# Moving VectorE work in the first and last quad of a gated cross-attention kernel

## The chip, the cores and the metric

The kernel runs on one core of a Trainium2 chip. The metric is the device time of one execution in microseconds, given as the median of several runs. A core has five engines that work side by side, each through its own instructions in order: TensorE (PE: matmuls, with the weight loads shown apart as PEld), VectorE (DVE), ScalarE (ACT), GpSimd (POOL) and SyncE (SP), which here issues most DMA transfers. They wait for each other by semaphores.

## The reference, cut to what matters

x holds 8 batches of 1024 rows with 1024 elements. The memory has 64 rows of 512 elements for each batch. All is float32.

```python
memory_proj = einsum('bme,de->bmd', memory, W_mem)
scores = einsum('bnd,bmd->bnm', x, memory_proj) / sqrt(D)
attn = softmax(scores, axis=-1)
memory_context = einsum('bnm,bmd->bnd', attn, memory_proj)
gate_input = concatenate([x, memory_context], axis=-1)
gate = sigmoid(einsum('bnf,df->bnd', gate_input, W_gate) + b_gate)
fused = x + gate * memory_context
out = fused * rsqrt(mean(square(fused)) + EPS) * norm_w
```

Softmax subtracts the row's maximum before the exponential. W1 below is the half of W_gate that meets x, W2 the half that meets the context.

## The kernel before, in words

**Tiling.** The 8192 rows of x are worked in 16 quads of 512 rows (four tiles of 128 rows, t = 0 to 3). A setup of about 80 us computes the projected memory and its product with W2 and stores both to DRAM. Then each quad multiplies its rows by W1 in a Strassen-like scheme with two levels: seven outer products, taken in ORDER 1, 6, 7, 5, 4, 2, 3 (line 613), each of seven inner products. An inner product is one call of `product` (line 866) and one slot, so a quad has 49 slots.

**One outer product** (`outer_product`, line 855) uses PSUM banks af and ed (two sets, in turn), and b and c. Its first inner product goes to af and is copied by ScalarE (line 876). The second, kB, goes to bank b and is drained by VectorE into u2. The third, kC, goes to bank c and is drained into u3. The fourth and fifth end in ed, drained into u4; the sixth and seventh in af. GpSimd's `pre` adds u3 and u4 to the gate tiles of 128x512, and VectorE's `fin_af` and `fin_ed` add the banks. L95 is the helper `tt` for all two-operand sums, L92 the helper of all matmuls, L98 that of SP's transfers.

**The visit.** Products 5 and 4, and products 2 and 3, form pairs. After kC of the second of a pair (4 or 3), TensorE makes a visit (line 796): the context itself and its part of the gate, for both of the pair, into banks b and c, two further banks, and af and ed. The first matmul of the visit needs bank b, so VectorE's drain of kB must have ended. After the visit come bank sums, the sigmoid on ScalarE, and the multiplication by the context (`gated`, or `last_gated` in the last quad, which also adds x from xl).

**Softmax.** In slot 10 `softmax_a` takes the row maximum on VectorE (line 429), multiplies it by -SCALE (line 430), and ScalarE takes four exponentials with that as bias. In slot 13 `softmax_b` takes a reciprocal on VectorE and scales on ScalarE. In slot 18 TensorE transposes the weights (line 451).

**Inner sums of W1.** For every outer product the weights have four sums (T1, T2, R12, T4, lines 214 to 216). Those of products 2 and 3 are not made in the setup: VectorE makes them in the first quad, in slots 3, 4, 5, 6 for product 2 and 12, 14, 16, 18 for product 3 (line 656). R12 is overwritten in place.

**The last quad.** Its tiles are finished by `last_square` (sum of squares, ScalarE), `last_root` (square root, ScalarE) and `last_norm`: a reciprocal on VectorE, one VectorE operation per half tile (multiply by the reciprocal root, multiply by norm_w), and a store of that half on SP. The list `when` (line 940) sets the slots for a pair: roots of tiles d and c, then norms (d, 0), (d, 1), (c, 0), (c, 1). For product 4 the tiles are d = 3 and c = 2; None stands for a place in the middle of product 3, right after its visit.

**Order.** The program is its own schedule: `at(slot, ...)` puts a step ahead of the inner product of that slot, `mid((quad, product), ...)` behind the bank sums that follow a visit, `mid((quad, product, 0), ...)` between the visit and these sums. `pin` keeps each engine's instructions in program order. An instruction that waits holds up all behind it on its engine.

Of the kernel before, what the change touches and what calls it, by code (L numbers as in the profile page):

```python
# [9 lines left out]
AF = mybir.ActivationFunctionType  # L10
ALU = mybir.AluOpType
# [9 lines left out]
def tile_gated_cross_attention_rmsnorm(  # L21
# [42 lines left out]
    nc = tc.nc  # L64
# [4 lines left out]
    NQ = B * QPB  # L69
# [3 lines left out]
    H = 512  # L73
    C = 256
    NPAIR = BM // P
    SCALE = 1.0 / float(D) ** 0.5
# [12 lines left out]
    pin = tc.keep_in_program_order  # L89
# [4 lines left out]
    def tt(eng, o, a, b, op):  # L94
        pin(eng.tensor_tensor(o, a, b, op))  # L95

    def load(o, i):
        pin(nc.sync.dma_start(o, i))  # L98

    def t4k(pool, shape, tag, name):  # L100
        return pool.tile(shape, F32, tag=tag, name=name)
# [31 lines left out]
    for k in range(KD):  # L133
        t = t4k(*((gpool, [P, D], "gate") if k < 7 else (apool, [P, D], "s4")), f"w2_{k}")
# [8 lines left out]
    nw_sb = const.tile([P, D], F32, name="nw_sb")  # L143
# [194 lines left out]
    A, S, L2, O = {}, {}, {}, {}  # L338
    sTs, attns, attnTs, scs, dens, mps, mgs = {}, {}, {}, {}, {}, {}, {}
    def where(q, t=0):  # L340
        return q // QPB, (q % QPB) * QT + t * P
# [84 lines left out]
    def softmax_a(q):  # L426
        sc = scs.pop(q)
        mx = t4k(small, [P, 4], "mx", f"mx{q}")
        pin(nc.vector.tensor_reduce(mx, sc, AX.X, ALU.max))
        pin(nc.vector.tensor_scalar(mx, mx, -SCALE, None, ALU.mult))  # L430
        e = attns[q] = t4k(small, [P, 4, M], "e", f"e{q}")
        den = dens[q] = t4k(small, [P, 4], "den", f"den{q}")
        for t in range(4):
            pin(
                nc.scalar.activation(
                    e[:, t], sc[:, t], AF.Exp, bias=mx[:, t : t + 1], scale=SCALE, accum_out=den[:, t : t + 1]
                )
            )
# [167 lines left out]
    def at(slot, fn, *args):  # L606
        due.setdefault(slot, []).append(lambda: fn(*args))

    def mid(key, fn, *args):
        beside.setdefault(key, []).append(lambda: fn(*args))  # L610
# [5 lines left out]
    def plan(q):  # L616
# [11 lines left out]
        at(t0 + (11 if q else 22), outer_s, q, 4)  # L628
        at(t0 + 9, transpose_scores, q)
        at(t0 + 10, softmax_a, q)  # L630
        at(t0 + 13, softmax_b, q)
        at(t0 + 18, transpose_attn, q)
# [20 lines left out]
    for o in (2, 3):  # L653
        w1_place(o)
    for i, (o, n) in enumerate((o, n) for o in (2, 3) for n in range(4)):
        at((3, 4, 5, 6, 12, 14, 16, 18)[i], inner_sum, nc.vector, o, n)
    slot = 0

    def step():
# [88 lines left out]
    def last_root(t):  # L748
# [5 lines left out]
            )  # L754
        )

    def last_norm(t, h):
        b, n0 = where(NQ - 1, t)
        rstd = halves[t][0][:, 2:3]
        if h == 0:  # L760
            pin(nc.vector.reciprocal(rstd, rstd))
        cols = slice(h * H, (h + 1) * H)
        g = O[NQ - 1, t][:, cols]
        pin(
            nc.vector.scalar_tensor_tensor(g, g, rstd, nw_sb[:, cols], ALU.mult, ALU.mult)  # L765
        )
        load(out[b, n0 : n0 + P, cols], g)

    def sqrt_table():

        t = t4k(small, [P, 1], "warm", "warm")
        pin(nc.scalar.activation(t, eps_sb, AF.Sqrt))
# [82 lines left out]
    def outer_product(q, o):  # L855
# [66 lines left out]
        if second:  # L922
            row, h, _ = EXT[o]
# [12 lines left out]
        if second and not nxt:  # L936
            c, d = 2 * row, 2 * row + 1
            if o == 3:
                sqrt_table()
            when = (3, 4, 5, 6, None, 11) if o == 4 else (0, 2, 2, 2, 3, 3)  # L940
            at(slot + when[0], last_root, d)
            at(slot + when[1], last_root, c)
            for w_, (t, h_) in zip(when[2:], ((d, 0), (d, 1), (c, 0), (c, 1))):
                if w_ is None:
                    mid((q, 3, 0), last_norm, t, h_)
                else:
                    at(slot + w_, last_norm, t, h_)
        elif second:

            c, d = 2 * row, 2 * row + 1  # L950
            for t in (d, c):
                at(slot + 5, residual, q, t)
            if row == 0:
                when = (17, 18, -1, None, 33, -2) if q + 2 < NQ else (17, 18, 20, 22, 24, 25)
            else:
                when = (17, 18, 22, 24, 29, 31)
            at(slot + when[0], square, q, c)
            at(slot + when[1], square, q, d)
            for w_, (t, h_) in zip(when[2:], ((c, 0), (c, 1), (d, 0), (d, 1))):
                if w_ is None:  # L960
                    mid((q + 1, 4), norm, q, t, h_)
                elif w_ < 0:
                    mid((q + 1, 4, 0) if w_ == -1 else (q + 1, 3), norm, q, t, h_)
                else:
                    at(slot + w_, norm, q, t, h_)
        del L2[q, o]

    for q in range(NQ):
        plan(q)
        for o in ORDER:  # L970
            outer_product(q, o)
# [29 lines left out]
```

## Time and profile before

| | us |
|---|---|
| median of 3 runs | 961.03 |
| the three runs | 960.99, 962.22, 961.03 |
| profiled execution | 961.78 |
| its span, first to last instruction | 960.0 |
| TensorE busy | 944.4 |
| VectorE busy | 817.3 |
| GpSimd busy | 712.2 |
| ScalarE busy | 366.3 |

Times in the timelines are microseconds from the first instruction: start, duration, engine, line of the kernel, operation, names of the output and inputs, shape, count, and in brackets how long the engine had been idle and what ended the idle time. Durations of neighbours overlap a little. A busy TensorE is not one at its peak, and the ends of matmuls are modelled. The first quad's products run from about 80 to 142 us, a later quad takes about 54 us, and the last matmul starts at 948.3.

### The profile page before, as it was taken

The page shows a single profiled execution, that of the slowest core. Times are in us where ns is not written, and L with a number is a line of the kernel's source. Part 1 is how long each engine was busy: PE and PEld are TensorE (multiplying, and loading weights), DVE is VectorE, ACT ScalarE, POOL GpSimd, SP SyncE. Part 2 cuts the span into 40 slices and gives each one's busy share as a digit, 9 for nine tenths or more (in the row PEclk, how much of TensorE's full clock was granted, in tenths as well). Part 3 has the DMA queues.
Part 4 walks back from the last instruction along what each step waited for, and adds up shares of the span by engine and source line. Part 5 has one row for each costly group of instructions (what it writes and reads, how often), then busy time and mean ns, then how long its engine had stood idle before and what let it go on. Part 6 is the DMA issues. An engine that isn't in the chain of part 4 may idle for free.

```text
span 960.0 us, 14298 instructions
## 1 busy us (share of the span) xinstructions
PE 944.4 (98%) x4984; PEld 777.6 (81%) x4984; DVE 817.3 (85%) x1260; ACT 366.3 (38%) x779; POOL 712.2 (74%) x778
## 2 busy tenths in 40 slices
PE   9999999999999999999999999999999999999994
PEld 7546788888888888888888888888888888888883
DVE  6989878888888888988888888988888888978887
ACT  3000335262433535262433535262433525262454
POOL 4997867788677777787677777777677877777681
PEclk9999999999999999999999999999999999999998
DMA  9866674481919365481919365481919365481712
GB/s 378 268 153 155 108 126 106 104 182 44 209 45 189 91 141 118 109 177 43 210 45 189 88 142 120 101 185 40 213 45 187 87 145 121 107 180 40 203 66 89
DMA packets 70919, 128.33 MB, mean 134 GB/s; under 512 B 12352, under 2 KB 49216, under 8 KB 70592
## 3 DMA queue, kind: packets, MB, share of 16 engines
q1 hardware_dynamic: 61664, 93.86, 37.0%
q0 software_dynamic: 9184, 33.56, 19.1%
q8 instruction: 40, 0.66, 0.3%
q14 instruction: 31, 0.25, 0.1%
HBM read 87.56 MB, written 41.68 MB: 135 GB/s over the span
## 4 chain that ended last, share of the span: by engine, by line
PE 92%; DVE 4%; ACT 1%; issue 1%; POOL 1%; DMA 1%; SPq 0%; POOLq 0%; DVEq 0%; ACTq 0%
PE af L92 28%; PE ed L92 19%; PE pc L92 11%; PE kC L92 9%; PE kB L92 9%; PE psT L92 6%; PE pg L92 5%; PE pm L92 2%; DVE gate L95 1%; DVE u L95 1%; DMA wm<-in_w_mem_t 1%; POOL l L95 0%; DVE gate L765 0%; DVE gate L699 0%; PE sc L420 0%
## 5 line engine op out<-in xcount | busy, mean ns | idle before, releaser
L95 POOL TENSOR_TENSOR gate<-gate,u 128x512 f32<-128x512 f32 (+1 forms) x224 | 248.9, 1123 | 193.9 <-DVE u L95 180.0
L670 ACT ACTIVATE gate<-gate 128x512 f32<-128x512 f32 x128 | 79.8, 630 | 184.2 <-DVE gate L95 184.2
L352 DVE STREAM_TRANSPOSE a<-xq 128x512 f32<-128x512 f32 x128 | 141.0, 1105 | 3.3 <-POOL it L95 3.3
L95 POOL TENSOR_TENSOR l<-a 128x256 f32<-128x256 f32 x128 | 111.9, 874 | 18.7 <-PE af L92 17.5
L699 DVE SCALAR_TENSOR_TENSOR gate<-gate,ss,nw_sb 128x512 f32<-128x512 f32 x120 | 120.7, 1007 | 1.1
L92 PE MATMUL pc<-mg,attnT 64*128 64x256 f32 x512 | 119.0, 383 | 2.2 <-DVE u L95 2.2
L92 PE MATMUL kB<-it,l 128*128 128x256 f32 x448 | 115.1, 379 | 0.5 <-DVE u L95 0.5
L92 PE MATMUL ed<-it,l 128*128 128x256 f32 x448 | 115.0, 379 | 0.0
L92 PEld LDWEIGHTS pc<-mg,attnT 64*128 64x128 f32 x512 | 93.2, 187 | 22.9 <-DVE u L95 13.0
L876 ACT COPY u<-af 128x256 f32<-128x256 f32 x112 | 40.7, 363 | 185.6 <-PE af L92 185.2
L95 DVE TENSOR_TENSOR gate<-gate,pc 128x512 f32<-128x512 f32 x113 | 76.0, 683 | 33.2 <-ACT gate L670 33.1
L92 PE MATMUL af<-w,a 128*128 128x256 f32 x384 | 98.5, 379 | 0.0
L92 PEld LDWEIGHTS kB<-it,l 128*128 128x128 f32 x448 | 85.1, 190 | 12.3 <-issue 0.8
L92 PEld LDWEIGHTS ed<-it,l 128*128 128x128 f32 x448 | 83.9, 190 | 10.7
L95 DVE TENSOR_TENSOR gate<-gate,ed 128x512 f32<-128x512 f32 x112 | 76.1, 680 | 14.4 <-POOL gate L95 14.3
L95 POOL TENSOR_TENSOR l<-s 128x256 f32<-128x256 f32 x96 | 85.1, 886 | 3.0 <-PE af L92 3.0
L92 PEld LDWEIGHTS af<-w,a 128*128 128x128 f32 x384 | 73.0, 190 | 10.3 <-issue 0.5
L95 DVE TENSOR_TENSOR gate<-gate,af 128x512 f32<-128x512 f32 (+1 forms) x128 | 76.0, 604 | 2.1 <-POOL gate L95 1.4
L92 PE MATMUL af<-mg,attnT 64*128 64x256 f32 x256 | 68.8, 389 | 0.0
L92 PE MATMUL ed<-it,a 128*128 128x256 f32 x256 | 67.4, 386 | 0.0
L684 ACT ACTIVATE junk<-gate 128x1024 f32<-128x1024 f32 x60 | 63.5, 1058 | 6.9 <-DMA gate<-in_x 6.0
L92 PE MATMUL af<-t,s 128*128 128x256 f32 x256 | 65.8, 380 | 0.0
(138 smaller groups left out, 1993.5 us busy)
## 6 DMA issues: line engine op xcount, KB each, us to landing
xq<-in_x SPq DMA_DIRECT2D x64, 512.0 KB, 10.4
gate<-in_x POOLq DMA_DIRECT2D x60, 512.0 KB, 8.5
out<-gate SPq DMA_DIRECT2D x60, 512.0 KB, 3.4
w<-in_w_gate_t SPq DMA_DIRECT2D x8, 512.0 KB, 10.2
w<-in_w_gate_t SPq DMA_DIRECT2D x2, 2048.0 KB, 16.1
mg<-mgd SPq DMA_DIRECT2D x16, 256.0 KB, 5.9
wm<-in_w_mem_t SPq DMA_DIRECT2D x4, 512.0 KB, 6.4
mpd<-mpT SPq DMA_DIRECT2D x4, 512.0 KB, 7.0
```

Of the source, the lines that this page charges most:

```text
L92: pin(nc.tensor.matmul(o, lhsT, rhs, start=start, stop=stop, skip_group_check=True))
L95: pin(eng.tensor_tensor(o, a, b, op))
L352: nc.vector.transpose(A[key][:, :, r * P : (r + 1) * P], chunks(xq[q][:, 4 * t : 4 * t + 4, :], KD)[:, half * KH : (half + 1) * KH],)
L670: pin(nc.scalar.activation(g, g, AF.Sigmoid))
L684: nc.scalar.activation(junk, O[q, t], AF.Square, accum_out=ss[:, t % 2 : t % 2 + 1])
L699: nc.vector.scalar_tensor_tensor(g[:, cols], g[:, cols], rstd[:, t % 2 : t % 2 + 1], nw_sb[:, cols], ALU.mult, ALU.mult,)
L876: pin(nc.scalar.copy(p1, af[:, 0]))
```

## The change

It has three parts. First, the multiplication of the row maximum by -SCALE goes from VectorE to ScalarE, in all 16 quads. Second, the four inner sums of W1 for product 3 in the first quad go from slots 12, 14, 16 and 18 to later places: two behind the bank sums after the visit of product 4, and two to slots 33 and 35. Third, in the last quad, tile 2 is multiplied by norm_w by GpSimd (a new step `last_weigh`, one instruction per half, between product 3's visit and the bank sums) and by its reciprocal root by ScalarE, in place of one VectorE operation per half. The new `when` takes the root of tile 2 and the norm (3, 0) in the same slot, puts the norm (3, 1) in the middle of product 3, where (2, 0) was, and the norm (2, 0) in slot offset 10.

```diff
-        pin(nc.vector.tensor_scalar(mx, mx, -SCALE, None, ALU.mult))
+        pin(nc.scalar.activation(mx, mx, AF.Copy, scale=-SCALE))
...
-        at((3, 4, 5, 6, 12, 14, 16, 18)[i], inner_sum, nc.vector, o, n)
+        if i in (4, 5):
+            mid((0, 4), inner_sum, nc.vector, o, n)
+        else:
+            at((3, 4, 5, 6, None, None, 33, 35)[i], inner_sum, nc.vector, o, n)
...
+    def last_weigh(t, h):
+        cols = slice(h * H, (h + 1) * H)
+        g = O[NQ - 1, t][:, cols]
+        tt(nc.gpsimd, g, g, nw_sb[:, cols], ALU.mult)
+
...
-        pin(
-            nc.vector.scalar_tensor_tensor(g, g, rstd, nw_sb[:, cols], ALU.mult, ALU.mult)
-        )
+        if t == 2:
+            pin(nc.scalar.activation(g, g, AF.Copy, scale=rstd))
+        else:
+            pin(
+                nc.vector.scalar_tensor_tensor(g, g, rstd, nw_sb[:, cols], ALU.mult, ALU.mult)
+            )
         load(out[b, n0 : n0 + P, cols], g)
...
-            when = (3, 4, 5, 6, None, 11) if o == 4 else (0, 2, 2, 2, 3, 3)
+            when = (3, 4, 4, None, 10, 11) if o == 4 else (0, 2, 2, 2, 3, 3)
+            if o == 4:
+                for h_ in range(2):
+                    mid((q, 3, 0), last_weigh, c, h_)
```

## The prediction

> **What bounds the kernel now.** I read the page first: busy times, the slices with the clock, then the chain of waits.
>
> ```profile
> span 960.0 us, 14298 instructions
> ...
> PE 944.4 (98%) x4984; PEld 777.6 (81%) x4984; DVE 817.3 (85%) x1260; ACT 366.3 (38%) x779; POOL 712.2 (74%) x778
> ```
>
> TensorE is busy for 944.4 of 960.0 us (98%), and its granted clock stands at 9 tenths or more in every slice but the last. Work taken from another engine pays only where TensorE waits for that engine, or after its last matmul. The TensorE timeline tells where. The first three rows are the first quad, the next two the second quad at the same place as reference, the last two the last quad. The bracket is idle time and its releaser.
>
> ```profile
> 109.87 1.10 PE L92 MATMUL kB<-it,l 128*128 128x256 f32 x4 [0.45 <-DVE u L95]
> 111.19 1.10 PE L92 MATMUL kC<-t,l 128*128 128x256 f32 x4 [0.21 <-DVE u L95]
> 112.75 0.48 PE L92 MATMUL pc<-mg,attnT 64*128 64x256 f32 x1 [0.46 <-DVE u L95]
> ...
> 164.98 1.03 PE L92 MATMUL kB<-it,l 128*128 128x256 f32 x4
> ...
> 166.80 0.48 PE L92 MATMUL pc<-mg,attnT 64*128 64x256 f32 x1
> ...
> 938.92 1.03 PE L92 MATMUL kC<-w,l 128*128 128x256 f32 x4
> 941.33 0.48 PE L92 MATMUL pc<-mg,attnT 64*128 64x256 f32 x1 [1.38 <-DVE u L95]
> ```
>
> Undisturbed, kB to visit takes 166.80 - 164.98 = 1.82 us. In the first quad the product before kB starts at 108.40, so kB was due 0.86 later at 109.26 and the visit at 111.08; it came at 112.75: **1.67 us lost**. In the last quad kC starts at 938.92, the visit was due 0.96 later (166.80 against kC's 165.84), at 939.88, and came at 941.33: **1.45 us lost**. From 113 to 923 no TensorE row carries such a wait. At 923.94 there is one of 0.34 us that the change does not touch.
>
> Next the VectorE timeline, what made it late: first quad, then last.
>
> ```profile
> 93.63 2.23 DVE L430 TENSOR_SCALAR mx<-mx 128x4 f32<-128x4 f32 x1
> ...
> 96.70 0.84 DVE L95 TENSOR_TENSOR it<-w 128x512 f32<-128x512 f32 x1
> ...
> 100.28 0.89 DVE L95 TENSOR_TENSOR it<-w,it 128x512 f32<-128x512 f32 x1
> ...
> 938.36 2.58 DVE L765 SCALAR_TENSOR_TENSOR gate<-gate,halves,nw_sb 128x512 f32<-128x512 f32 x2
> ...
> 941.91 1.79 DVE L765 SCALAR_TENSOR_TENSOR gate<-gate,halves,nw_sb 128x512 f32<-128x512 f32 x1
> ...
> 946.32 0.75 DVE L765 SCALAR_TENSOR_TENSOR gate<-gate,halves,nw_sb 128x512 f32<-128x512 f32 x1
> ```
>
> The four sums of W1 for product 3 (first and last shown, the others at 98.12, 0.68 us, and 99.35, 0.69 us) and the factor stand ahead of the drain of kB at 109.31. In the last quad two norms stand ahead of the drain at 940.86 that frees the visit's bank, and a third ahead of the bank sums at 943.61. From there VectorE works almost without a gap to its last norm at 955.78.
>
> [...] the norm at 941.91 takes 1.79 us with GpSimd's 1.27 us sum started at 941.88, and 0.75 us at 946.32 with GpSimd idle. The factor on 128x4 takes 2.23 us between GpSimd sums. [...] the trace has loads of 1.28 us. [...] the copy of line 876 runs at 903.34, after a Sqrt, with no load before it.
>
> **The change, part by part.**
>
> First quad, removed from ahead of the late drains: the factor's 2.23 us and four sums, 0.84 + 0.68 + 0.69 + 0.89 = 3.10 us. That is 5.3 us, but waits for data take a part. My replay of VectorE's order: u4 of product 6 must wait for its matmuls (about 94.5). The next sum waits for GpSimd's 128x512 sum, done at about 95.5[...]. u4 of product 7 waits for TensorE at 100.8. Then the transposes (next x landed by 87.7 + 12.2 = 99.9) and the rest follow, and the drain of kB of product 5 comes at 107.2 instead of 109.31. The lead of 2.1 us exceeds the 1.67 us needed; product 4's kB is then drained as soon as TensorE delivers it. Take 1.67; at the low end, [...]1.0.
>
> Where the sums go: two stand behind the four bank sums of product 4's visit, ahead of the two multiplications by pc of product 5 (116.73). They cost 0.7 to 1.3 us each. Those multiplications free banks b and c for product 2's kB and kC, TensorE at 120.98 and 121.85. With TensorE 1.67 us earlier and the multiplications done near 117.4, over 2 us remain before 119.3 and 120.2. The other two sums fall where VectorE already waits 0.69 and 0.70 us for a sigmoid (120.50, 122.49). All four are read only in product 3, from about 125. Cost: nothing, with that cover; without it, at most the 3.1 us again.
>
> The factor on ScalarE, 16 times: VectorE loses 0.78 us a quad (2.23 in the first), ScalarE gains 0.2 to 0.3 us (a 128x1 activation takes 0.29 at 931.15). ScalarE idles about 3.9 us before it in each later quad (58.6 us in 15 waits), so nothing is queued behind. The table load then follows the new instruction instead of VectorE's, and the exponentials start 0.5 us earlier. TensorE does not wait here: 0 us on the path from the second quad on.
>
> Last quad. One norm of tile 3 moves ahead of u4 of product 2, the other behind product 3's visit; both norms of tile 2 leave VectorE. Ahead of the late drain stands one norm instead of two. It starts beside GpSimd's sum at 938.00, so I price it 0.75 to 1.79 us against 2.50 for two (938.36 to 940.86): the drain comes 0.7 to 1.75 us earlier, TensorE can use at most 1.45. At the visit one norm replaces a reciprocal and a norm: 0.2 us more. Later the 946.32 norm goes (0.66 from start to start) and tile 2's reciprocal comes back (0.2). VectorE reaches the last bank sum (949.55) 0.7 + 0.2 + 0.46 = 1.4 to 1.45 + 0.2 + 0.46 = 2.1 us earlier. TensorE's last product ends 0.85 us before that sum and moves up too, so it sets no later end.
>
> Cover for the new work: GpSimd weighs twice at 1.27 us (its price at 941.88) in its 5.65 us of idleness ahead of 948.79. ScalarE scales twice at 0.63 (a 128x512 sigmoid)[...], in gaps of 0.88 and 0.94 us before 946.43 and 948.42. Behind the second scaling wait a square and the sigmoid of 949.38: about 0.1 us may be late. [...] I take 1.6 for the tail, 0.5 to 2.2 with these. The stores on SP keep their order; tile 2's come earlier than the last tile's, which alone lie at the end.
>
> Sum: 1.67 + 1.6 = 3.3 us. The profiled span 960.0 becomes 956.7. The profiled execution took 961.78 in all, 1.8 outside its span, and the median of the runs is 961.03: predicted 961.03 - 3.3 = **957.7 us**.
>
> **The rivals.**
> Only one place yields (0.20). For: VectorE's margins are small; after the repair the drain before the visit has only some 0.3 us. Against: 5.3 us are removed for a need of 1.67. Time 961.03 minus 1.4 to 1.7: 959.3 to 959.6, or 958.8 if half of the other comes too.
> No gain (0.09). [...] Against: the weighing has to end only by 948.79. Time 960.3 to 961.5.
> Slower (0.06). The factor on ScalarE lengthens softmax. In the second quad ScalarE's last scaling ends at 154.76, and TensorE's transposes of the weights follow at 155.26, weights loaded at 155.04: a margin of 0.28 us, 15 times. It decides once the chain grows by more than 0.28 us. A second table load in each quad would do so: 1.28 + 0.29 - 0.78 - 0.28 = 0.5 us times 15 = 7.6, less 3.3: 965.3 us. Against: copies after Sqrt and Exp in this trace need no load.
>
> **How the numbers follow.** Both places repaired has 0.65, with its own range 956.7 to 958.7 (1.67 + 2.2 at best, and 0.4 us for run-to-run scatter; 1.0 + 1.4 at worst). Change below 0.2%, 1.9 us, is what a measurement of this kernel cannot tell from none: faster ends at 959.1, slower begins at 963.0. Faster: 0.65 plus half the one-place case, 0.75. Same: the other half and no gain, 0.19. Slower 0.06. The range 956.7 to 959.7 takes in both places and one.
>
> **What would show it.** TensorE rows at kB, kC and the visit of the first quad, about 109.3 to 111.1, without brackets; the last visit within 2.2 us of its kB. If kB still waits there, my replay of the lead is wrong. The transposes of line 451 without a wait, and table loads no more than now. GpSimd's two weighings ended before its last sum; the last bank sum 3.1 to 3.8 us earlier than 949.55. The prediction is wrong if new TensorE waits stand near 119 to 125 or in every quad.

## The result, and the profile after

The changed kernel takes a median of 958.3 us (six runs, 957.75 to 958.74), the kernel before in six runs on the same chip 961.51 (960.99 to 962.22). The ratio is 0.9966, 95% interval 0.9955 to 0.9976: 3.2 us less, 3.3 were forecast. The forecast of 957.7 started from 961.03, so the median lies 0.6 above it. The profiled execution after took 957.75 us, span 956.0. The two spans lie 4.0 us apart, more than the medians; the run "The kernel before once more" shows why.

The page after: span and busy times, the shares of the chain that ended last, and one group of matmuls.

```profile
span 956.0 us, 14301 instructions
...
PE 943.6 (99%) x4984; PEld 778.2 (81%) x4984; DVE 811.4 (85%) x1242; ACT 371.0 (39%) x797; POOL 717.3 (75%) x780
...
PE 97%; DVE 1%; DMA 1%; ACT 0%; issue 0%; POOL 0%; SPq 0%; DVEq 0%
...
L92 PE MATMUL pc<-mg,attnT 64*128 64x256 f32 x512 | 119.0, 383 | 0.3 <-DVE u L95 0.3
```

TensorE's share of the chain is 97%. VectorE lost the 16 factors and two norms (1260 to 1242 instructions), ScalarE gained those 18. The matmuls of the visits wait 0.3 us for VectorE in the whole kernel: that is the untouched wait at product 4's visit in the last quad.

The TensorE timeline after, at the rows that carried brackets before: first quad, then last quad.

```profile
109.08 1.03 PE L92 MATMUL kB<-it,l 128*128 128x256 f32 x4
109.95 1.03 PE L92 MATMUL kC<-t,l 128*128 128x256 f32 x4
110.90 0.48 PE L92 MATMUL pc<-mg,attnT 64*128 64x256 f32 x1
...
937.07 1.03 PE L92 MATMUL kC<-w,l 128*128 128x256 f32 x4
938.03 0.48 PE L92 MATMUL pc<-mg,attnT 64*128 64x256 f32 x1
```

None of these rows waits. kB to visit takes 110.90 - 109.08 = 1.82 us, as in the undisturbed quad that the prediction read.

The VectorE timeline after: the drain of kB of product 5 in the first quad, then the tail of the last quad.

```profile
107.26 0.42 DVE L95 TENSOR_TENSOR u<-u,kB 128x256 f32<-128x256 f32 x1
...
935.39 1.79 DVE L776 SCALAR_TENSOR_TENSOR gate<-gate,halves,nw_sb 128x512 f32<-128x512 f32 x1
...
937.43 0.41 DVE L95 TENSOR_TENSOR u<-u,kB 128x256 f32<-128x256 f32 x1
...
938.48 0.75 DVE L776 SCALAR_TENSOR_TENSOR gate<-gate,halves,nw_sb 128x512 f32<-128x512 f32 x1
...
945.51 0.69 DVE L95 TENSOR_TENSOR gate<-gate,af 128x512 f32<-128x512 f32 x1 [0.75 <-PE af L92]
```

In the last quad one norm stands ahead of the drain (937.43), and the last bank sum (945.51) now waits 0.75 us for TensorE's last product.

To compare runs I measured distances in each trace: from the first matmul of the first quad's first outer product to the first visit; between the last two visits (product 4's and 3's of the last quad); and from the last visit to the last bank sum and to the end of the span. All in us, one execution each. The ends of matmuls are modelled, so only starts of matmuls are used.

| kernel | first visit | between last two visits | last bank sum | end |
|---|---|---|---|---|
| before, profile shown | 32.77 | 17.39 | 8.22 | 18.67 |
| before, profiled again | 32.78 | 16.61 | 8.23 | 18.69 |
| after | 31.10 | 15.94 | 7.48 | 17.92 |
| sums alone | 31.10 | 16.62 | 8.24 | 18.72 |
| factor alone | 32.61 | 16.62 | 8.23 | 18.68 |
| sums and factor | 31.10 | 16.61 | 8.23 | 18.68 |
| last quad alone | 32.69 | 15.94 | 7.48 | 17.94 |
| new order, no hand-over | 31.10 | 15.94 | 8.08 | 18.55 |
| hand-over, old order | 31.10 | 17.40 | 9.69 | 20.12 |
| one half tile more handed over | 31.10 | 15.94 | 7.66 | 18.12 |

### The profile page after: what moved, and what is told of

Read it like the earlier page. It is cut to its first block, busy times and chain, and to the rows that moved or that the text cites. A ratio compares the mean times of both kernels' runs of the same rounds, so it can differ in the third digit from the quotient of the medians.

```text
span 956.0 us, 14301 instructions
## 1 busy us (share of the span) xinstructions
PE 943.6 (99%) x4984; PEld 778.2 (81%) x4984; DVE 811.4 (85%) x1242; ACT 371.0 (39%) x797; POOL 717.3 (75%) x780
## 4 chain that ended last, share of the span: by engine, by line
PE 97%; DVE 1%; DMA 1%; ACT 0%; issue 0%; POOL 0%; SPq 0%; DVEq 0%
PE af L92 30%; PE ed L92 21%; PE pc L92 12%; PE kC L92 10%; PE kB L92 10%; PE psT L92 6%; PE pg L92 5%; PE pm L92 2%; DMA wm<-in_w_mem_t 1%; PE pa L451 0%; PE sc L420 0%; DVE gate L702 0%; DVE gate L776 0%; DVE u L95 0%; DVE gate L95 0%
## 5 line engine op out<-in xcount | busy, mean ns | idle before, releaser
L95 POOL TENSOR_TENSOR gate<-gate,u 128x512 f32<-128x512 f32 (+1 forms) x224 | 243.2, 1098 | 184.4 <-DVE u L95 148.5
L702 DVE SCALAR_TENSOR_TENSOR gate<-gate,ss,nw_sb 128x512 f32<-128x512 f32 x120 | 115.6, 964 | 1.1
L95 POOL TENSOR_TENSOR l<-s 128x256 f32<-128x256 f32 x96 | 78.4, 817 | 3.0 <-PE af L92 3.0
L95 DVE TENSOR_TENSOR u<-u,kC 128x256 f32<-128x256 f32 x112 | 45.9, 410 | 23.8 <-PE kC L92 20.3
```

The costliest lines, as they stand in the source:

```text
L702: nc.vector.scalar_tensor_tensor(g[:, cols], g[:, cols], rstd[:, t % 2 : t % 2 + 1], nw_sb[:, cols], ALU.mult, ALU.mult,)
```

## The experiments

The medians of the kernel before, on the same chip as each run, lie between 961.27 and 961.45 us. Each run below names its own ratio to it.

**The sums alone.** The kernel before with the new places for the four sums, nothing else:

```diff
-        at((3, 4, 5, 6, 12, 14, 16, 18)[i], inner_sum, nc.vector, o, n)
+        if i in (4, 5):
+            mid((0, 4), inner_sum, nc.vector, o, n)
+        else:
+            at((3, 4, 5, 6, None, None, 33, 35)[i], inner_sum, nc.vector, o, n)
```

> Only the four inner sums of W1 for product 3 move, as in the change; factor and last quad as before. My theory: the sums (3.1 us) make most of VectorE's lateness, since the factor's 2.23 us partly overlap waits for data. The drain of kB of product 5 comes 1.6 to 2.0 us earlier than 109.31, TensorE's three waits in the first quad vanish, time -1.5 us (-1.2 to -1.7). Rival, both edits are needed because GpSimd and TensorE data set the pace: -0.8 us or less, with a wait left at the visit. The last visit stays at 1.45 us late in both.

Measured: 959.78 us, ratio 0.998 (0.9971 to 0.9989), 1.5 us less. Its TensorE timeline, where the three waits stood:

```profile
109.59 1.03 PE L92 MATMUL kB<-it,l 128*128 128x256 f32 x4
110.45 1.03 PE L92 MATMUL kC<-t,l 128*128 128x256 f32 x4
111.41 0.48 PE L92 MATMUL pc<-mg,attnT 64*128 64x256 f32 x1
```

The first visit comes 31.10 us after the quad's first matmul: the whole 1.67 us is back with the sums alone.

**The factor alone.**

```diff
-        pin(nc.vector.tensor_scalar(mx, mx, -SCALE, None, ALU.mult))
+        pin(nc.scalar.activation(mx, mx, AF.Copy, scale=-SCALE))
```

> Only the factor moves to ScalarE, in all quads. My theory: the sums then fill the idle time that the factor left[...], so the lead is about 0.7 us: one or two of the three waits in the first quad remain, time -0.7 us (-0.3 to -1.2). In later quads nothing on TensorE: the transposes of line 451 get 0.6 us more room. Rival, the factor alone is the cause: -1.7 us. Rival, a longer softmax chain: TensorE waits at line 451 in each quad, time +7 us.

Measured: 961.06 us, ratio 0.9996 (0.9988 to 1.0005). Its TensorE timeline still has all three waits:

```profile
109.54 1.10 PE L92 MATMUL kB<-it,l 128*128 128x256 f32 x4 [0.27 <-DVE u L95]
110.86 1.10 PE L92 MATMUL kC<-t,l 128*128 128x256 f32 x4 [0.21 <-DVE u L95]
112.43 0.48 PE L92 MATMUL pc<-mg,attnT 64*128 64x256 f32 x1 [0.47 <-DVE u L95]
```

A miss: 0.7 us was expected, the first visit comes 0.16 us earlier, and the median can't be told from no change. Its VectorE timeline where the factor stood, and the first of the four sums:

```profile
94.41 0.42 DVE L95 TENSOR_TENSOR u<-u,ed 128x256 f32<-128x256 f32 x1 [0.97 <-PE ed L92]
95.73 0.69 DVE L95 TENSOR_TENSOR gate<-gate,ed 128x512 f32<-128x512 f32 x1 [0.90 <-POOL gate L95]
96.33 1.27 DVE L95 TENSOR_TENSOR it<-w 128x512 f32<-128x512 f32 x1
```

Of the 2.23 us taken away 0.97 comes back as a wait for TensorE and 0.90 as one for GpSimd. The four sums then took 1.27, 1.24, 0.88 and 0.68 us, 4.07 together against 3.10 before. These three outweigh the 2.23 us; a little is left because a later wait of VectorE for GpSimd shrinks from 1.51 to 0.83 us.

**Both first-quad parts.**

> Factor and sums move, last quad as before. My theory: -1.7 us, no TensorE wait in the first quad, last visit still 1.45 us late. Together with the run of the last quad alone this should sum to the whole change (about -3.2 us) if the two places are independent; if the first place's gain were lost on the way, this run would be at 0.

Measured: 959.36 us, ratio 0.9975 (0.9966 to 0.9985), 1.9 less; first visit at 31.10, as with the sums alone. In the two profiled executions 0.18 us of the difference lies in the setup (the quad's first matmul stands at 80.31 with the sums alone, at 80.13 here); the rest of the 0.4 us between the medians is not tied to a place in the traces, and I take it for scatter.

**The last quad alone.** The changed kernel with the factor and the sums as before.

> Only the last quad's part: order of norms, GpSimd weighing, ScalarE scaling. My theory: from the trace of the changed kernel, TensorE's last visit 1.45 us earlier and the last bank sum 2.2 us earlier, time -2.2 us (the prediction's term was -1.6, its range -0.5 to -2.2). The three waits of the first quad stay at 1.67 us. Rival, the tail is worth only the 1.5 that the medians leave after the first quad: -1.5 us.

Measured: 959.88 us, ratio 0.9984 (0.9976 to 0.9992), 1.4 less, not the 2.2 expected. Against the repeated profile of before, the last visit comes 16.61 - 15.94 = 0.67 us earlier and the end 18.69 - 17.94 = 0.75 nearer to it: 1.42. With both first-quad parts' 1.9 the medians add up to 3.3, against 3.2 for the whole change, so the two places are independent within the scatter.

**The kernel before once more**, unchanged.

> The kernel before, unchanged, for a second trace. In the profile of before, VectorE's first add of xl in the last quad took 1.84 us[...]; in the five other traces the same two operations start as close and VectorE goes first, 0.69 us. If that is an even race of one place, this trace has VectorE first, the visits of products 4 and 3 lie 16.6 us apart (17.4 in the profile of before), and the last visit is 0.7 us late in place of 1.45. If the old program always loses it: 17.4 again.

It took 961.17 us, span 959.4, and shows where the missing 0.8 us went. Its last visit waits 0.60 us where it waited 1.38 in the profile of before:

```profile
940.71 0.48 PE L92 MATMUL pc<-mg,attnT 64*128 64x256 f32 x1 [0.60 <-DVE u L95]
```

The cause shows in the timelines of VectorE and GpSimd in the last quad, first in the profile of before that the prediction read:

```profile
928.53 1.84 DVE L95 TENSOR_TENSOR gate<-gate,xl 128x512 f32<-128x512 f32 x1
928.54 1.27 POOL L95 TENSOR_TENSOR gate<-gate,u 128x512 f32<-128x512 f32 x1
```

Then in the second execution of the same kernel:

```profile
928.69 0.69 DVE L95 TENSOR_TENSOR gate<-gate,xl 128x512 f32<-128x512 f32 x1
928.72 1.79 POOL L95 TENSOR_TENSOR gate<-gate,u 128x512 f32<-128x512 f32 x1
```

The same two operations start within 0.03 us of each other. In the first execution GpSimd's sum takes 1.27 us and VectorE's addition of xl 1.84, in the second GpSimd's takes 1.79 and VectorE's 0.69. Where VectorE loses, that is, where its addition is the long one, the last visit comes 17.39 - 16.61 = 0.78 us later. So the 1.45 us wait that the prediction wanted to recover was 0.67 us of order and 0.78 us of what happened in that one execution. VectorE won in 10 of the 14 traces of this study. The two spans differ by more than the medians for this reason: 959.998 - 955.953 is 4.05, and 4.05 - 0.78 = 3.27 us, of which 0.18 lies in the setup (79.98 against 79.80). The six runs of before fit: three at 960.99 to 961.25 and three at 961.78 to 962.22, with a median between the two groups. Only one of them, at 961.78, has a trace, so the groups are not shown to be the two outcomes.

**The new order without the hand-over.** The changed kernel, but tile 2's norms stay on VectorE, at the new places in `when`:

```diff
-            if o == 4:
-                for h_ in range(2):
-                    mid((q, 3, 0), last_weigh, c, h_)
...
-        if t == 2:
-            pin(nc.scalar.activation(g, g, AF.Copy, scale=rstd))
-        else:
-            pin(
-                nc.vector.scalar_tensor_tensor(g, g, rstd, nw_sb[:, cols], ALU.mult, ALU.mult)
-            )
+        pin(
+            nc.vector.scalar_tensor_tensor(g, g, rstd, nw_sb[:, cols], ALU.mult, ALU.mult)
+        )
```

> The whole change but for the hand-over of tile 2: its norms stay on VectorE, one operation per half, at the new places in the order. My theory: the new order alone repairs the last visit (its first matmul within 1.85 us of kB's), but VectorE carries two operations of 0.66 us more before the last bank sum[...]: last bank sum 0.3 to 0.6 us later after the visit than in the changed kernel (7.48), time -2.7 us against before. Rival, the hand-over is what matters: -1.7 us, as with the first quad alone.

Measured: 958.86 us, ratio 0.997 (0.996 to 0.9979), 2.4 less. The visit is on time (15.94), so the order repairs it. The last bank sum stands 8.08 after it, not 7.48: two norms of 0.75 and 0.74 us are back ahead of the drain that GpSimd's last sum needs. The hand-over is worth these 0.60 us (0.56 by the medians).

**The hand-over with the old order.** One line of the changed kernel undone:

```diff
-            when = (3, 4, 4, None, 10, 11) if o == 4 else (0, 2, 2, 2, 3, 3)
+            when = (3, 4, 5, 6, None, 11) if o == 4 else (0, 2, 2, 2, 3, 3)
```

> The whole change but for the order of the norms: tile 2 is weighed by GpSimd and scaled by ScalarE, both norms of tile 3 stay ahead of product 3's drain of kB. My theory: the last visit is 0.7 us late again (16.6 us after product 4's), and from there TensorE's last product sets the end as in the changed kernel: last bank sum 7.5 us after the visit. Time -2.4 us against before, 0.7 us behind the changed kernel. Rival, VectorE's load alone counts and not the order: as the changed kernel, -3.1 us.

Measured: 961.12 us, ratio 0.9998 (0.999 to 1.0007): a miss, since nearly all is lost, the first quad's gain included. Its ScalarE timeline:

```profile
937.23 0.35 ACT L887 COPY u<-af 128x256 f32<-128x256 f32 x1
...
943.06 0.72 ACT L773 ACTIVATE gate<-gate,halves 128x512 f32<-128x512 f32 x1 [5.47 <-POOL gate L95]
943.80 1.28 ACT L673 ACT_TABLE_LOAD   x1
945.09 1.15 ACT L673 ACTIVATE gate<-gate 128x512 f32<-128x512 f32 x2
```

With the old places ScalarE's scaling of tile 2 stands ahead of the sigmoids, and waits for GpSimd's weighing; behind it stand the table load and two sigmoids, and VectorE waits 3.05 us for those. The last bank sum comes 9.69 us after the visit. With both first-quad parts, the old order and no hand-over the time was 959.36 us, so at this place the hand-over costs 1.8 us. In this trace VectorE also lost the addition of xl (1.83 us), so of the visit's lateness 0.78 us is that again.

**The slower rival's price.** Six copies by 1.0 added to softmax's chain in every quad of the changed kernel:

```diff
         pin(nc.scalar.activation(mx, mx, AF.Copy, scale=-SCALE))
+        for _ in range(6):
+            pin(nc.scalar.activation(mx, mx, AF.Copy, scale=1.0))
```

> The changed kernel with six more ScalarE multiplications of the row maximum by 1.0 in each quad, each waiting for the one before; the output is the same. This tests the mechanism of the slower rival. The factor takes 0.20 us, so the chain grows by 1.2 to 1.5 us; the margin ahead of the weight load of line 451 is 0.92 us in the changed kernel. If softmax is that close to the path, TensorE waits 0.3 to 0.6 us in each of 15 quads: +4 to +9 us on the changed kernel, 962 to 967 us. If it is not, the time stays at 958.3.

Measured: 962.84 us, ratio 1.0016 (1.0009 to 1.0023), 4.5 us over the changed kernel. The transposes' weight loads (line 453 of that kernel, 451 before) now wait for the scaling in 15 quads (waits: total, count, longest):

```profile
PEld pa L453 <- ACT e L446: 5.1, 15, 0.3
```

The chain grew by six times 0.236 = 1.42 us and TensorE is held up by 0.29 (later visits 54.34 us apart instead of 54.05). So the chain could grow by 1.42 - 0.29 = 1.13 us before it cost anything. That is also what the trace of the changed kernel leaves in the second quad between the end of the scaling (152.29) and the first matmul of the transposes (153.42).

**Without cover.** The four moved sums ahead of product 4's drains in the changed kernel:

```diff
-        if i in (4, 5):
-            mid((0, 4), inner_sum, nc.vector, o, n)
-        else:
-            at((3, 4, 5, 6, None, None, 33, 35)[i], inner_sum, nc.vector, o, n)
+        at((3, 4, 5, 6, 28, 28, 28, 28)[i], inner_sum, nc.vector, o, n)
```

> The changed kernel with all four inner sums of product 3 in slot 28, right ahead of product 4's drains of kB and kC, where VectorE has no slack in the changed kernel. My theory: this is the price without the cover. The drain of product 4's kB ends some 3 us later, TensorE's visit comes 2.5 to 3.1 us late, time 2.5 to 3.1 us above the changed kernel, about 961. Rival, other slack in the first quad takes them up: less than 1 us above.

Measured: 965.15 us, ratio 1.0039 (1.0025 to 1.0053), 6.85 over the changed kernel: a miss, by more than twice. Its VectorE timeline first, the four sums beside GpSimd's own:

```profile
110.58 0.69 DVE L95 TENSOR_TENSOR it<-w 128x512 f32<-128x512 f32 x1
111.30 1.64 DVE L95 TENSOR_TENSOR it<-w,it 128x512 f32<-128x512 f32 x1
112.86 1.20 DVE L95 TENSOR_TENSOR w<-w 128x512 f32<-128x512 f32 x1
113.99 1.21 DVE L95 TENSOR_TENSOR it<-w,it 128x512 f32<-128x512 f32 x1
```

GpSimd's four sums of 128x512 run from 109.42 to 114.65 beside them. VectorE's take 4.74 us in place of 3.10, and the visit comes 35.44 - 31.10 = 4.34 us late. Its TensorE timeline from there, the last of kC and three matmuls of the visit:

```profile
110.29 1.03 PE L92 MATMUL kC<-t,l 128*128 128x256 f32 x4
...
115.59 0.79 PE L92 MATMUL pc<-mg,attnT 64*128 64x256 f32 x1 [4.27 <-DVE u L95]
...
116.17 0.63 PE L92 MATMUL pc<-mg,attnT 64*128 64x256 f32 x1
...
116.60 0.63 PE L92 MATMUL pc<-mg,attnT 64*128 64x256 f32 x1
```

And the same kernel's table of four stretches: length, busy time of TensorE, its weight loads, VectorE, ScalarE and GpSimd, the granted clock, the DMA share, GB/s.

```profile
110.00:115.00 5.00, 1.32 (x7) 0.81 (x5) 4.97 (x6) 1.36 (x2) 5.00 (x5) 0.87 0.87 147
115.00:118.00 3.00, 2.41 (x12) 1.98 (x14) 1.17 (x4) 0.00 (x0) 2.92 (x5) 0.50 0.23 45
118.00:121.00 3.00, 3.00 (x20) 2.43 (x18) 2.02 (x4) 1.26 (x2) 1.17 (x1) 0.57 0.00 0
121.00:124.00 3.00, 3.00 (x19) 2.38 (x16) 1.81 (x4) 0.00 (x0) 0.00 (x0) 1.00 0.00 0
```

After 4.27 us of idleness the granted clock stands at 0.50 (115 to 118). With one step from 1.00 to 0.50 and one back, an estimate, the means of 0.87 and 0.57 put the fall near 113.7, 2.4 us after the last kC matmul ended (111.32, modelled), and the return near 120.6. Matmuls of the visit start 0.42 us apart instead of 0.21, from 115.59 to 120.44; half of these 4.85 us is lost. The next visit of the same kind stands 56.50 us away instead of 54.05, 2.45 us more. 4.34 + 2.45 = 6.79 us, the measured 6.85.

**Can more be handed over?** In the changed kernel half 0 of tile 0 is weighed by GpSimd and scaled by ScalarE too; this is the edit. In a second kernel half 0 of tile 1 is as well, weighed in slot offset 12.

```diff
-        if t == 2:
+        if t == 2 or (t, h) == (0, 0):
...
+                at(slot + 11, last_weigh, 0, 0)
```

> The changed kernel with the same treatment for the first half of tile 0, the last tile to be normed: GpSimd weighs it after tile 2, ScalarE scales it at the end. VectorE's last row of five (reciprocal, four norms) loses one norm of 0.67 us. My theory: the last VectorE operation and the end come 0.5 to 0.67 us earlier after the last visit (17.92 in the changed kernel), time -0.6 us on the changed kernel. Rival, the weighing delays GpSimd's last sum past TensorE's last product, or the store on SP waits for ScalarE: no gain.

> As the kernel before it, and the first half of tile 1 too, weighed behind GpSimd's last sum. ScalarE then does two scalings of 0.72 us at the very end and VectorE two norms. My theory: the end comes 0.2 us earlier than with one half, set by ScalarE. Rival, [...]later than with one half.

Measured: 958.63 us, ratio 0.9971 (0.996 to 0.9981), and 958.89, ratio 0.9974 (0.9965 to 0.9984). Both miss: no gain over 958.3. In the first, VectorE's last norm ends 13.96 us after the last visit instead of 14.45, yet the end moves from 17.92 to 18.12. The weighing, 1.73 us long, delays GpSimd's last sum and with it the last bank sum (7.66 instead of 7.48). And the end follows the stores. SP issues the last four, of 256 KB each, in the changed kernel and then in this one:

```profile
950.33 2.55 SPq L98 DMA_DIRECT2D out<-gate  x4
...
951.53 2.37 SPq L98 DMA_DIRECT2D out<-gate  x4
```

They land at 952.65, 953.68, 954.30 and 954.93 in the changed kernel and at 953.87, 954.87, 955.51 and 956.14 here: one after the other, the last three 0.62 to 0.64 us apart. The span ends 5.6 us after the first of the four is issued in both (956.0 and 957.2), as it does before (954.37 and 960.0). So an earlier last norm brought nothing here, where the first of the four was issued no earlier. With two halves handed over VectorE's last norm ends at 13.39 and the span at 18.67 us after the visit, as that first store then waits for ScalarE (issued at 951.50, 13.05 after the visit, against 12.30 in the changed kernel).

**The last wait left.** The 0.34 us wait at product 4's visit in the last quad goes when the last norm of the quad before is put later:

```diff
-                when = (17, 18, -1, None, 33, -2) if q + 2 < NQ else (17, 18, 20, 22, 24, 25)
+                when = (17, 18, -1, None, 33, -2) if q + 2 < NQ else (17, 18, 20, 22, 24, 33)
```

> The changed kernel with one further norm moved: the last of the quad before, one of two that stand ahead of the drain of product 4's kB in the last quad, goes nine slots later, into a wait of VectorE for a sigmoid. My theory: the one TensorE wait left in the last quad (visit of product 4, 0.67 us after the last kC matmul where 0.31 is undisturbed) goes, -0.36 us on the changed kernel: two equal visits of the last two quads lie 54.05 us apart in place of 54.41. Rival, VectorE has no room nine slots later and the last visit or the last bank sum comes as much later: no gain.

Measured: 958.4 us, ratio 0.9963 (0.995 to 0.9977). The wait is gone from the trace (visits 54.05 us apart instead of 54.41), but in that execution VectorE lost the addition of xl (1.76 us) and the last visit came 0.45 us late. In the median nothing of the 0.36 us is to be seen. One trace can't tell whether moving that norm makes GpSimd win more often, so why the gain is missing from the median stays open.

## Why the prediction came out as it did

**First quad: right.** The visit came at 31.10 instead of 32.77, 1.67 us. That this fits to the hundredth is no merit of the replay: TensorE can use no more than 1.67, and any larger lead gives the same. The lead was a little smaller than replayed. The late drain came at 107.26 (107.2 replayed), but the quad's first matmul stands at 79.80 here and at 79.98 before; counted from there the drain is 1.87 us earlier, not 2.1. The low end of 1.0 that the prediction gave was an estimate of its author. What the prediction left open inside this step is the weight of the two parts. It counted 2.23 us of factor and 3.10 us of sums as one lead; the factor alone yields 0.16 us of the 1.67, the sums alone all of it.

**The moved sums cost nothing: right.** Two of them took 0.91 and 1.10 us behind product 4's bank sums, the others 0.83 and 0.80 where VectorE had waited for sigmoids. The multiplications by pc were done at 118.0 (VectorE's pair at 116.74, 1.27 us), against 117.4 in the forecast, and no TensorE row from 117 to 124 waits. The price without cover was wrong: "at most the 3.1 us again" was 6.85. The step took the durations from their old places, where they met other GpSimd sums (there they took 3.10 us, ahead of product 4's drains 4.74), and left out the lower clock (0.50; 2.45 us).

**The factor on ScalarE: right on the path.** The ScalarE timeline after, second quad:

```profile
148.16 0.20 ACT L430 ACTIVATE mx<-mx 128x4 f32<-128x4 f32 x1 [3.03 <-DVE mx L429]
148.39 1.28 ACT L435 ACT_TABLE_LOAD   x1
```

0.20 us were expected as 0.2 to 0.3; table loads number 65 before and after. The chain moved up a little more than forecast (0.63 for 0.5 us), and from the second quad on nothing on TensorE follows from it.

**The slower rival's threshold was mis-sized.** The prediction put it at 0.28 us, from ScalarE's end to the weight load. The run with longer chains shows that the next matmul counts: 1.13 us of growth were free after the change. The same reading of before, the end of the scaling at 154.76 against the matmul at 155.26, is 0.50 us. By this count, an estimate that no run tests, a second table load in each quad would have cost 7.6 less 0.22 times 15, 4.3 us, before the gain is taken off. With 3.3 off that is 962.0: slower than before, but short of the 963.0 that the prediction set for "slower", and not its 965.3.

**The last quad: the mechanism right, the size a little off, and one sentence wrong.** The term was 1.6 us; alone it measured 1.4 by the medians, 1.42 by the trace. The sum of places is 1.67 + 1.42 = 3.09 us against 3.2 measured. The step read "1.45 us lost" from one execution, of which 0.78 was the lost addition of xl. The norm ahead of the drain took 1.79 us, the dear end of its range, which by the prediction's own sum leaves 0.7. That the term came near is in part luck: with 0.2 + 0.46 for what follows the visit, where 0.75 came, its 1.6 us counted some 0.9 for the visit, where 0.67 was to be had. The sentence that TensorE's last product "sets no later end" was wrong: it ends (by the model) 7.38 us after the visit in every kernel, and the last bank sum now waits for it at 7.48. VectorE already idles for 0.75 us before that sum, so cutting its work further would gain nothing there.

**GpSimd and ScalarE: cover as said.** GpSimd's weighing in the timeline after, and ScalarE's scalings:

```profile
940.32 2.96 POOL L95 TENSOR_TENSOR gate<-gate,nw_sb 128x512 f32<-128x512 f32 x2
```

```profile
941.62 0.72 ACT L773 ACTIVATE gate<-gate,halves 128x512 f32<-128x512 f32 x1 [0.19 <-POOL gate L95]
...
943.31 0.72 ACT L773 ACTIVATE gate<-gate,halves 128x512 f32<-128x512 f32 x1
```

The weighing took 1.48 us each, not 1.27, and ended at 943.28, ahead of GpSimd's last sum at 944.24. Beside it ran VectorE's additions of xl, one of which took 1.05 instead of 0.69 us; in the run with the old order, where VectorE waited beside it for most of the time, the two weighings took 2.50 us together, not 2.96. The scaling took 0.72 us each, 0.09 more than the 0.63 us sigmoid of the same size. The run with the old order shows what the prediction didn't ask: the cover held only where the scaling stands behind the sigmoids (958.3 us against 961.12).

**The rivals.** "Only one place yields" and "no gain" (VectorE waiting beside GpSimd as long as before, the author's estimate) fell with the first and the last quad each measured alone (1.9 us with both parts, 1.5 with the sums, and 1.4); both ratios' intervals lie below 1.

## What to carry to other kernels

A wait read from one execution has to be split into what order makes and what only that execution shows before it is counted as a gain. A second profile of the unchanged kernel showed it here, but VectorE lost in 4 of 14 traces, so two profiles can also agree by chance. An operation that goes to another engine needs two places checked, who stands behind it on the new engine and which of its inputs is late: here the hand-over is worth 0.6 us behind the sigmoids, and costs more than it gives ahead of them. When TensorE has no wait left, look for the next cap at once: here they are the last product and the stores at the end, and further hand-overs gained nothing.

## What the runs showed of the hardware that was not expected

- **A long wait cost twice.** After 4.27 us of TensorE idleness the granted clock stood at 0.50 (the sums without cover, 115 to 118), and the next visit came another 2.45 us late. By the estimate above the clock fell about 2.4 us after the last matmul; the matmuls then started 0.42 us apart for 4.85 us. A wait of 1.39 us (last visit with the hand-over in the old order) shows no such fall: from 940.29 on its matmuls start 0.21 or 0.22 us apart.
- **Two operations side by side, and not always the same one long.** VectorE's addition of xl took 0.69 us in 10 traces and 1.76 to 1.84 in the other four; GpSimd's sum beside it took 1.27 us in the profile of before and 1.79 in the repeated one. Which of the two starts first doesn't sort the traces. VectorE's addition starts 0.01 us ahead of GpSimd's sum in the profile of before and loses, 0.03 ahead with the hand-over in the old order and loses, 0.02 or 0.03 ahead in the ones after and repeated, and wins; with the last wait moved GpSimd's sum starts 0.06 ahead, and VectorE loses. Losing cost 0.78 us in the old order of the norms; in the new one it cost 0.64 (the sums without cover) and 0.45 (the last wait moved).
- **A short factor that took long.** VectorE's multiplication of 128x4 numbers took 2.23 us in the first quad, beside GpSimd's sums, and 0.78 in the median of the 16 quads; on ScalarE, after the change, it took 206 ns in the mean of 16. In the second quad of before it ended at 150.79, as GpSimd's sum of 128x512 beside it did (150.77).
